# Two cross-attention layers on one core: both Gram products in the middle of a slot, a fixed order for some GpSimd work, and the image values' load and mask at other places

## The chip, the cores and the metric

The kernel runs on one core of one Trainium2 chip. Its time is the device time of one execution in microseconds (us); the time before is the median of three runs. The profile is one further execution, recorded instruction by instruction. The engines are named as the profile names them: PE (TensorE, matmuls; PEld is its weight load), DVE (VectorE), ACT (ScalarE), POOL (GpSimd), SP (SyncE, which issues most DMAs).

## The reference

Two cross-attention layers over a batch of 16 sequences, 256 tokens of 320 channels, 20 heads of 16. The second layer's input is the first layer's output; both attend to the same context (256 tokens of 512 channels per sequence), whose last tokens are "image" tokens with keys and values of their own. Layer 2, which the change is about, cut to what matters:

```python
q = heads(x @ W_q)                       # x: layer 1's output
k_t, v_t = heads(text @ W_k), heads(text @ W_v)     # text: 252 context tokens
probs_t = softmax(q @ k_t.T * 0.25)
text_out = probs_t @ v_t
k_ip, v_ip = heads(ip @ W_k_ip), heads(ip @ W_v_ip) # ip: the last 4 context tokens
qsem = l2norm(probs_t @ text)            # a 512-vector per head and query
sem = qsem @ l2norm(ip).T
probs_ip = softmax(q @ k_ip.T * 0.25 + 0.5 * sem) * spatial_mask
out = (text_out + probs_ip @ v_ip) @ W_out + b_out + x
```

The kernel doesn't form `qsem`. It needs only its norm and its products with the image tokens, and gets both from Gram products of the context: the norm is `p G p`, with `G` the 256 x 256 product of the context with itself and `p` the unnormalized probabilities, and the products with the image tokens are columns of the same `G`.

## The kernel before, in words

Layer 2 goes over 80 slots, `k = NS .. 2*NS - 1` with `NS = 80`: five slots (groups of four heads) for each of the 16 sequences, here called batches. In what follows `n` is the first slot of a batch. Layer 1 fills the 80 slots before in a like manner.

One slot of layer 2 (`slot1`) issues, in this order:

- `both1(k, 0)`: the transposed scores of slot k for the first half of the keys (L788), the plain scores of slot k+2 (L793), whose maximum DVE takes (L794) and whose image columns it copies (L810), and the exponentials on ACT (L800).
- `attend1(k - 2)`: probabilities times values (L861), then the norm's row through a matrix of zeros and ones, the "zone" matmuls (L863), which read the finished norm sum; then `settle1` (L906 to L914).
- `both1(k, 1)`: the same for the second half.
- `norm1(last, 0, 0)`, with `last = k - 1`: four matmuls of the Gram matrix with rounded probabilities (L848) and their product with the low part on DVE (L851).
- side work due by a third of the slot.
- `norm1(last, 0, 1)`, `rounded1(k, 0)`, the loads of a later slot's score operands, `norm1(last, 1, 0)`, `norm1(last, 1, 1)`, `rounded1(k, 1)`: together ten more norm matmuls. Each pair's two products are summed (L853) by POOL for the first pair (`u = 0`) and by DVE for the second. `rounded1` rounds the exponentials of one pair on ACT (L838) and subtracts on POOL (L839) what was rounded off: the "low halves", two of them for each pair. The rounded copies lie in a ring of two buffers, so the copy of slot k takes the place of that of slot k - 1, which the norm matmuls read.
- side work due by two thirds, the maxima's way into the score operands (L826, L828, L830), and side work due by the slot's end.

The side work lies in generators (`task(key, times, ...)`): each has a list of times in slots, and `fill(now)` runs all steps that are due, earliest time first. Those that matter here, with their times against the batch's first slot n:

- `t1`, `tokens1`: two steps for the values (L212), and then one for each of two Gram products of twelve matmuls (also L212, 128x256), with copies by ACT (L487, L488; L493, L494, L498) and DVE (L486, L489; L492, L495, L499). Times -3.67, -3, -2.67, -2.33; a step beyond the list takes the last time.
- `o1`, `open1`: a batch's queries. It loads layer 1's output and splits it into rounded and low parts (`split`: ACT L509, POOL L510, DVE L511) at -7, and projects it (L520 on `hq`) from -6.67 on. L510 is queued. In slots that is the same place at which the batch ahead has just done its Gram products.
- `k1`, `keys1`: a batch's keys, with low parts of the context on POOL (L148 on `cta`), also queued.
- `i1`, `image_softmax`: the image tokens' softmax over all groups of a batch at once, in ten steps from 6.67 to 8.33. Its last lines load the image values of the batch (`vb`, 4 rows of 384, sent to 32 partitions at once; shown as `rs<-vipd`), transpose the probabilities (L960) and multiply `vb` with a mask (L961). `vb` is one tile for all batches.
- `c1`, `close1`: image probabilities times `vb` (L968), the sum with the text part (L969), the output projection (L520 on `ho`) and the store.

Two things set the order of instructions on an engine. PE's order is the program's, as written. For DVE, ACT, POOL and SP a planner in the compiler plays the program through with its own durations and picks, whenever an engine is free, the earliest written instruction that is ready by its reckoning; what waits on a load or on PE can so be overtaken by later work, or later work be put into a gap. Two helpers bind that order: `anchor(inst)` makes `inst` its engine's anchor, replacing the one before, and `queued(inst)` orders `inst` behind its engine's present anchor, without a wait for its result. On the engine itself the order is then fixed, and an instruction that waits holds those behind it.

Of the kernel before, what the change touches and what calls it, by code (L numbers as in the profile page):

```python
# [21 lines left out]
CP = 384  # L22
E = 512
T0 = 77
NIP = 4
# [5 lines left out]
NG = H // 4  # L31
# [10 lines left out]
def RAMP(t):  # L42
    return t if t < -5 or t > 3 else (t + 5) * 0.375
# [5 lines left out]
def xattn2(  # L49
# [27 lines left out]
    nc = tc.nc  # L77
    f = lambda ap: ap.bitcast(F32)
    mm = nc.tensor.matmul

    def dma(out, in_):
        nc.sync.dma_start(*(f(ap) if ap.dtype == FR else ap for ap in (out, in_)))
# [16 lines left out]
    def buf(tag, shape, dtype=F32, bufs=1, name=None):  # L99
        if tag in ("wB", "wD", "vr", "raw"):  # L100
            return sb.tile(shape, dtype, tag=tag, name=name or tag, bufs=bufs)
        size = 1
        for d in shape[1:]:
            size *= d
        if tag not in slots:
            slots[tag] = [0, dtype] + [const_tile([128, max(size, words.get(tag, 0))], f"{tag}_{i}", dtype) for i in range(bufs)]
        n, kind, *ring = slots[tag]
        assert kind == dtype and len(ring) == bufs, tag
        slots[tag][0] += 1
        t = ring[n % bufs][: shape[0], :size]  # L110
        names = "abcd"[: len(shape) - 1]
        if len(names) > 1:
            t = t.rearrange(f"p ({' '.join(names)}) -> p {' '.join(names)}", **dict(zip(names, shape[1:])))
        return t
# [5 lines left out]
    vipd = dram.tile([BI, CP], F32, name="vipd")  # L120
# [11 lines left out]
    def queued(inst, *behind):  # L132

        for other in behind or [anchors.get(inst.ins.engine)]:
            if other is not None:
                tc.add_manual_dep(
                    inst.ins, other.ins.name, mybir.DependencyInfo(mybir.DependencyClass.NoSync, mybir.DependencyReason.DATA), reason="order"
                )
        return inst

    def anchor(inst):
        anchors[inst.ins.engine] = inst
        return inst
# [228 lines left out]
    w1, v1t, gmt = {}, [], []  # L372
# [98 lines left out]
    def tokens1(b):  # L471
        ct = ct1[b]
        V, G = v1t[b % 2], gmt[b % 2]
        vc = vcols(V, V1W)
        for t, lo, sc in ((0, 0, 1.0), (1, DUP, tmask[:, 2:3])):
            vp = bank()[:, :320]
            prod(vp, lambda s, k: ct(s, k)[:, lo : lo + 128], w1["v"], 4)
            nc.scalar.activation(vc[:, t, :, 0:16], vp.rearrange("p (h d) -> p h d", d=D), AF.Copy, scale=sc)
            yield
        rnb = rn[:, 4 * b : 4 * b + 4].unsqueeze(1).to_broadcast([128, H, NIP])  # L480
        for t, lo in ((0, 0), (1, DUP)):
            g = bank()[:, :S]
            prod(g, lambda s, k: ct(s, k)[:, lo : lo + 128], ct, 4)
            ip = g[:, T1:S].unsqueeze(1).to_broadcast([128, H, NIP])
            if t == 0:
                nc.vector.tensor_mul(vc[:, 0, :, 17:21], ip, rnb)  # L486
                nc.scalar.copy(G[:, 0, :], g[:, 0:128])  # L487
                nc.scalar.copy(G[:, 1, 4:], g[:, 128:T1])  # L488
                nc.vector.tensor_sub(G[:, 4, :], g[:, 0:128], f(G[:, 0, :]))  # L489
            else:  # L490
                tm = tmask[:, 2:3]
                nc.vector.scalar_tensor_tensor(vc[:, 1, :, 17:21], ip, tm, rnb, op0=ALU.mult, op1=ALU.mult)  # L492
                nc.scalar.activation(G[:, 2, :], g[:, 0:128], AF.Copy, scale=tm)  # L493
                nc.scalar.activation(G[:, 3, 4:], g[:, 128:T1], AF.Copy, scale=tm)  # L494
                nc.vector.scalar_tensor_tensor(  # L495
                    G[:, 5, :], g[:, 0:128], tm, f(G[:, 2, :]), op0=ALU.mult, op1=ALU.subtract
                )
                nc.scalar.activation(G[:, 5, :], f(G[:, 5, :]), AF.Copy, scale=2.0)  # L498
                nc.vector.scalar_tensor_tensor(  # L499
                    G[:, 6, 4:], g[:, 128:T1], tm, f(G[:, 3, 4:]), op0=ALU.mult, op1=ALU.subtract  # L500
                )
            yield
        return V, G
# [100 lines left out]
    QK, P, W, R = {}, {}, {}, {}  # L604
# [229 lines left out]
    def rounded1(k, u):  # L834
        R[k, u] = buf("ctb", [128, 2, 2, S], FR, bufs=SIZES["CTB"], name="ph")
        W[k, u] = buf("wB", [128, 2, 2, S], bufs=SIZES["WB"], name="wt")
        for t in range(2):
            nc.scalar.activation(R[k, u][:, t], P[k, u][:, t], AF.Copy, scale=0.5)  # L838
            anchor(nc.gpsimd.tensor_sub(W[k, u][:, t], P[k, u][:, t], f(R[k, u][:, t])))  # L839

    blocks = (((0, 0), (2, 1), (4, 0), (5, 1)), ((1, 0), (3, 1), (6, 1)))

    def norm1(k, u, n):

        gm = get("t1", k // NG - B)[1]
        yp = bank().rearrange("p (h t) -> p h t", h=2)
        for i, (gb, kt) in enumerate(blocks[n]):
            mm(yp, gm[:, gb], R[k, u][:, kt], start=i == 0, stop=i == len(blocks[n]) - 1)  # L848
        w = W[k, u]
        product = yp if n and u else w[:, n]  # L850
        nc.vector.tensor_mul(product, yp, w[:, n])  # L851
        if n:
            (nc.vector if u else nc.gpsimd).tensor_add(w[:, 0], w[:, 0], product)  # L853

    def attend1(k):
        b, g = divmod(k - NS, NG)
# [60 lines left out]
    def image_softmax(b, lo=0, hi=NG):  # L917

        gs, n = slice(lo, hi), hi - lo
        nt, si = norms[b][:, gs], results["si", b]  # L920
        pool = nc.gpsimd
        small = lambda n, t: buf(t, [128, NG, 8] + ([n] if n > 1 else []))[:, gs]

        u = small(1, "u")
        pool.tensor_mul(u, nt[:, :, :, 0], nt[:, :, :, 0])
        yield
        nc.vector.scalar_tensor_tensor(u, u, EPS2 / 4, nt[:, :, :, 5], op0=ALU.mult, op1=ALU.max)
        yield
        r = small(1, "r")

        nc.scalar.activation(r, u, AF.Ln, scale=2.0**20)
        nc.scalar.activation(r, r, AF.Exp, bias=w1["shift"], scale=-0.5)
        yield
        b4 = lambda t: t.unsqueeze(3).to_broadcast([128, n, 8, NIP])
        a = small(NIP, "a")
        pool.tensor_mul(a, nt[:, :, :, 1:5], b4(r))
        by_group = lambda t: t[:, :, : NG * NIP].rearrange("p f (g n) -> p g f n", n=NIP)[:, gs]
        pool.tensor_add(a, a, by_group(si))
        yield
        m4 = small(1, "m4")  # L940
        nc.vector.tensor_reduce(m4, a, axis=AX.X, op=ALU.max)
        yield
        pool.tensor_sub(a, a, b4(m4))
        yield
        nc.scalar.activation(a, a, AF.Exp, scale=SCALE)
        yield
        z4 = small(1, "z4")
        nc.vector.tensor_reduce(z4, a, axis=AX.X, op=ALU.add)
        nc.vector.reciprocal(z4, z4)
        yield  # L950
        pool.tensor_mul(z4, z4, mk.unsqueeze(1).to_broadcast([128, n, 8]))
        pi = w1["pip"]
        pool.tensor_mul(by_group(pi), a, b4(z4))
        if hi < NG:
            return
        vb = w1["vb"]
        dma(vb, vipd[NIP * b : NIP * (b + 1)].unsqueeze(0).to_broadcast([32, NIP, CP]))
        yield
        pT = w1["pT"]
        nc.vector.transpose(pT, pi.rearrange("p f c -> p (f c)"))  # L960
        nc.vector.tensor_mul(vb, vb, w1["bmask"])  # L961
        return pT, vb

    def close1(b):
# [28 lines left out]
    def task(key, times, make, *needs):  # L993
        tasks[key] = [times, 0, make, needs, len(tasks)]
# [38 lines left out]
    def shifted(n, *times):  # L1033

        return [RAMP(n + t) for t in times]
# [10 lines left out]
    for c in range(B // 2):  # L1046
        n, k = 10 * c, [("k0", c)] if c else []
# [11 lines left out]
    for b in range(B):  # L1059
        n = NS + 5 * b  # L1060
        task(("k1", b), shifted(n, -7, -6.67, -6.33, -5.67, -5, -4.67), lambda b=b: keys1(b), ("w2",), *([("t1", b - 1)] if b else []), *([("w4", 1)] if b > 2 else []))
        task(("t1", b), shifted(n, -3.67, -3, -2.67, -2.33), lambda b=b: tokens1(b), ("k1", b), ("w3", b % 2))
        task(("o1", b), shifted(n, -7.67, -7, -6.67, -5.33, -4.33, -4), lambda b=b: open1(b), ("w7",), ("c0", b), *([("o1", b - 1)] if b else []))
        task(("i1", b), shifted(n, 6.67, 6.67, 6.67, 6.67, 7.33, 7.33, 7.67, 7.67, 8, 8.33), lambda b=b: image_softmax(b, NG - 1 if b == B - 1 else 0), ("gathered", b), ("taken", B + b - 1), *([("i1a",)] if b == B - 1 else []))
        task(("c1", b), shifted(n + (1.67 if b > B - 3 else 0), 8.67, 9.33, 9.67, 10.33, 11.67, 13.33), lambda b=b: close1(b), ("i1", b), ("w4", 1))
# [160 lines left out]
```

## Time and profile before

| | |
|---|---|
| time, median of 3 runs | 1523.62 us (1520.76 to 1527.41) |
| the profiled execution: time, span | 1525.5 us, 1523.4 us |
| granted TensorE clock, mean | 0.987 |
| PE, PEld busy | 95%, 79% |
| DVE, ACT, POOL busy | 77%, 63%, 75% |
| second half, 760 to 1523 us: PE, POOL, DVE busy | 736.09, 577.18, 635.40 us |
| the longest waits by line | POOL L839 for ACT L838 167.5 us, POOL L679 for ACT L676 161.1 us |

The span is cut into what each engine was busy with; idle time of an engine is put down to what ended it. Rows of the instruction view give the start, the duration, the engine, the line, the operation, the tile written and the tiles read, then in brackets the idle time before and what released it. Rows of the chain give start, duration, engine, tile and line. A row of the waits gives the total, the times it happened and the longest. Matmul ends are modelled. Layer 2's batches repeat with a period of 51.8 us.

### The profile page before, as it was taken

Reading aid. Unit: us, or ns where it says so; the run is one execution under the profiler, and the core shown is the slowest. Engines: PE = TensorE matmul, PEld = TensorE weight load, DVE = VectorE, ACT = ScalarE, POOL = GpSimd, SP = SyncE. Lnnn points to the kernel's source line nnn. Section 1 sums busy time; section 2 is a strip of 40 time slices with the busy share of each in tenths; the row PEclk is TensorE's granted clock in tenths of the full one; section 3 lists DMA queues with packets and bytes.
Section 4 is the critical chain, followed back from the end, with each engine's and each line's share of the span. In section 5 each row is a group of like instructions: output and inputs, shape, how many; then the busy total and the mean of one; then the engine's idle time right before and its main releaser. Section 6 shows DMA issues by size and latency. Waiting matters only on the chain.

```text
span 1523.4 us, 35306 instructions
## 1 busy us (share of the span) xinstructions
PE 1452.4 (95%) x12522; PEld 1196.4 (79%) x12522; DVE 1180.6 (77%) x2584; ACT 956.0 (63%) x2073; POOL 1142.2 (75%) x1161
## 2 busy tenths in 40 slices
PE   7799999999999999799999999999999999999997
PEld 6788888888888878577777877777777777777765
DVE  5467676767676777777888888888888888788896
ACT  5557676767676866656656556656665665556563
POOL 3259797979797967787778678767877787778785
PEclk9899999999999999899999999999999999999999
DMA  6666565656565665465424443443444343434311
GB/s 217 165 176 175 163 175 163 175 162 175 163 175 163 168 182 136 104 188 171 156 86 138 121 139 115 127 130 109 136 117 138 108 144 110 150 98 120 115 42 59
DMA packets 226971, 215.38 MB, mean 141 GB/s; under 512 B 49714, under 2 KB 210708, under 8 KB 226796
## 3 DMA queue, kind: packets, MB, share of 16 engines
q1 hardware_dynamic: 225056, 211.83, 48.4%
q8 instruction: 100, 1.64, 0.5%
q10 hardware_dynamic: 1740, 1.30, 0.3%
q14 instruction: 75, 0.61, 0.2%
HBM read 122.17 MB, written 89.49 MB: 139 GB/s over the span
## 4 chain that ended last, share of the span: by engine, by line
PE 72%; POOL 10%; DVE 6%; DMA 5%; issue 3%; ACT 3%; SPq 0%; ACTq 0%; POOLq 0%; DVEq 0%
PE X L212 21%; PE X L848 14%; PE X L520 10%; PE P L711 7%; POOL wt L839 6%; PE S L650 5%; PE T L673 4%; PE T L788 3%; DMA rs<-vipd 3%; PE P L861 2%; DVE mn L794 2%; PE S L793 2%; POOL wt L853 2%; PE P L863 1%; PE X L569 1%
## 5 line engine op out<-in xcount | busy, mean ns | idle before, releaser
L679 POOL TENSOR_TENSOR P<-P,rs 128x512 f32<-128x512 f32 x320 | 411.4, 1307 | 161.3 <-ACT P L676 161.1
L839 POOL TENSOR_TENSOR wt<-P,ctb 128x512 f32<-128x512 f32 x212 | 271.0, 1292 | 117.7 <-ACT ctb L838 117.7
L848 PE MATMUL X<-ctb,gm 128*128 128x512 f32 x1120 | 293.7, 402 | 0.0
L676 ACT ACTIVATE P<-T 128x512 f32<-128x512 f32 x320 | 174.8, 593 | 106.2 <-PE T L673 99.1
L848 PEld LDWEIGHTS X<-ctb,gm 128*128 128x128 f32 x1120 | 199.5, 188 | 46.4 <-issue 0.4
L794 DVE TENSOR_REDUCE mn<-S 128x4 fp32r<-128x1008 f32 x160 | 191.6, 1197 | 31.3 <-PE S L793 31.3
L851 DVE TENSOR_TENSOR wt<-X,wt 128x512 f32<-128x512 f32 x240 | 164.2, 685 | 31.1 <-PE X L848 30.1
L800 ACT ACTIVATE P<-T 128x512 f32<-128x512 f32 x212 | 114.8, 593 | 47.7 <-PE T L788 47.2
L838 ACT ACTIVATE ctb<-P 128x512 fp32r<-128x512 f32 x212 | 124.2, 625 | 32.0 <-PE X L848 30.5
L652 DVE TENSOR_REDUCE mn<-S 128x4 fp32r<-128x716 f32 x160 | 142.5, 891 | 0.0
L711 PE MATMUL P<-P,vr 128*32 128x256 f32 x1920 | 126.9, 395 | 5.3 <-DVE mx L575 2.8
L520 PE MATMUL X<-hq,wE 128*128 128x256 f32 x768 | 114.4, 292 | 4.7 <-ACT hq L509 3.5
L520 PE MATMUL X<-ho,wF 128*128 128x256 f32 x768 | 108.6, 284 | 4.8 <-DVE ho L752 4.0
L212 PE MATMUL X<-cta,wA 128*128 128x252 f32 (+1 forms) x720 | 105.4, 290 | 7.3 <-ACT wA L147 5.8
L520 PEld LDWEIGHTS X<-hq,wE 128*128 128x128 f32 x768 | 103.6, 194 | 9.1 <-ACT hq L509 4.0
L520 PEld LDWEIGHTS X<-ho,wF 128*128 128x128 f32 x768 | 102.0, 190 | 9.9 <-DVE ho L752 4.4
L839 POOL TENSOR_TENSOR wt<-qsl,ctb 128x512 f32<-128x512 f32 x54 | 69.2, 1293 | 51.9 <-ACT ctb L838 49.8
L853 POOL TENSOR_TENSOR wt<-wt 128x512 f32<-128x512 f32 x80 | 103.3, 1292 | 0.0
L212 PEld LDWEIGHTS X<-cta,wA 128*128 128x128 f32 x720 | 93.8, 194 | 11.9 <-ACT wA L147 6.1
L722 DVE STREAM_TRANSPOSE nt<-P 128x512 f32<-128x512 f32 x80 | 57.1, 713 | 51.9 <-PE P L711 51.9
L147 ACT CAST kst<-X 128x252 fp32r<-128x252 f32 (+3 forms) x94 | 35.1, 373 | 95.3 <-PE X L212 75.5
L711 PEld LDWEIGHTS P<-P,vr 128*32 128x32 f32 x1920 | 56.5, 112 | 46.6 <-issue 9.6
(217 smaller groups left out, 3383.2 us busy)
## 6 DMA issues: line engine op xcount, KB each, us to landing
qd<-q SPq DMA_DIRECT2D x96, 384.0 KB
kd<-kst SPq DMA_DIRECT2D x73, 256.0 KB
rawc<-in_cT_dram SPq DMA_DIRECT2D x60, 256.0 KB
ks<-kd SPq DMA_DIRECT2D x160, 96.0 KB
qs<-qd SPq DMA_DIRECT2D x160, 96.0 KB
qs<-qd SPq DMA_DIRECT2D x60, 192.0 KB
ks<-kd SPq DMA_DIRECT2D x60, 192.0 KB
kd<-kst SPq DMA_DIRECT2D x21, 512.0 KB
```

Source lines behind the costliest of these rows:

```text
L212: last = mm(out, lhs(a, k), rhs(b, k), start=i == 0, stop=i == len(terms) - 1)
L520: mm(pp, w(s, k, slice(m * 128, (m + 1) * 128)), a[:, t], start=i == 0, stop=i == len(terms) - 1)
L652: anchor(nc.vector.tensor_reduce(mn[:, t, 1], sp[:, :, T0:], axis=AX.X, op=ALU.max))
L676: exp = anchor(nc.scalar.activation(pt, st[p], AF.Exp, scale=SCALE))
L679: anchor(nc.gpsimd.tensor_mul(pt, pt, rs[:, t : t + 1].to_broadcast([128, 2, S])))
L711: mm(pv[32 * s : 32 * s + 32, o : o + S], v[:, vt, h : h + 32], P[k, s // 2][:, t, s % 2], start=vt < 2, stop=vt != 1,)
L794: anchor(nc.vector.tensor_reduce(maxes[k + 2][:, t], sp[:, :, :T1], axis=AX.X, op=ALU.max))
L838: nc.scalar.activation(R[k, u][:, t], P[k, u][:, t], AF.Copy, scale=0.5)
L839: anchor(nc.gpsimd.tensor_sub(W[k, u][:, t], P[k, u][:, t], f(R[k, u][:, t])))
L848: mm(yp, gm[:, gb], R[k, u][:, kt], start=i == 0, stop=i == len(blocks[n]) - 1)
L851: nc.vector.tensor_mul(product, yp, w[:, n])
L853: (nc.vector if u else nc.gpsimd).tensor_add(w[:, 0], w[:, 0], product)
```

## The change

The second Gram product of a batch is issued directly after the first, in the middle of slot n-3 (time -2.67 instead of -2.33), so that both stand ahead of the ten norm matmuls of that slot instead of one on each side. The low halves of the second pair (`u = 1`) are queued on POOL, and POOL's norm sum becomes an anchor. The load of the image values is written into the first step of `image_softmax` instead of ahead of its last, and their mask multiplication is queued on DVE.

```diff
@@ rounded1 @@
-            anchor(nc.gpsimd.tensor_sub(W[k, u][:, t], P[k, u][:, t], f(R[k, u][:, t])))
+            low = nc.gpsimd.tensor_sub(W[k, u][:, t], P[k, u][:, t], f(R[k, u][:, t]))
+            anchor(queued(low) if u else low)
@@ norm1 @@
         if n:
-            (nc.vector if u else nc.gpsimd).tensor_add(w[:, 0], w[:, 0], product)
+            total = (nc.vector if u else nc.gpsimd).tensor_add(w[:, 0], w[:, 0], product)
+            if not u:
+                anchor(total)
@@ image_softmax, ahead of its first step @@
+        vb = w1["vb"]
+        if hi == NG:
+            dma(vb, vipd[NIP * b : NIP * (b + 1)].unsqueeze(0).to_broadcast([32, NIP, CP]))
@@ image_softmax, its end @@
         if hi < NG:
             return
-        vb = w1["vb"]
-        dma(vb, vipd[NIP * b : NIP * (b + 1)].unsqueeze(0).to_broadcast([32, NIP, CP]))
         yield
         pT = w1["pT"]
         nc.vector.transpose(pT, pi.rearrange("p f c -> p (f c)"))
-        nc.vector.tensor_mul(vb, vb, w1["bmask"])
+        queued(nc.vector.tensor_mul(vb, vb, w1["bmask"]))
         return pT, vb
@@ the tasks @@
-        task(("t1", b), shifted(n, -3.67, -3, -2.67, -2.33), lambda b=b: tokens1(b), ...
+        task(("t1", b), shifted(n, -3.67, -3, -2.67, -2.67), lambda b=b: tokens1(b), ...
```

More of the change, by code (lines that the diff above doesn't have):

```diff
@@ L1061, in xattn2 @@
         task(("k1", b), shifted(n, -7, -6.67, -6.33, -5.67, -5, -4.67), lambda b=b: keys1(b), ("w2",), *([("t1", b - 1)] if b else []), *([("w4", 1)] if b > 2 else []))
-        task(("t1", b), shifted(n, -3.67, -3, -2.67, -2.33), lambda b=b: tokens1(b), ("k1", b), ("w3", b % 2))
+        task(("t1", b), shifted(n, -3.67, -3, -2.67, -2.67), lambda b=b: tokens1(b), ("k1", b), ("w3", b % 2))
         task(("o1", b), shifted(n, -7.67, -7, -6.67, -5.33, -4.33, -4), lambda b=b: open1(b), ("w7",), ("c0", b), *([("o1", b - 1)] if b else []))
```

## The prediction

> **What bounds the kernel now.** I read the page first (busy shares, then the chain), then a window of one steady batch of layer 2, the chain of waits inside it, the waits by line, and last the instructions in order of time.
>
> ```profile
> PE 1452.4 (95%) x12522; PEld 1196.4 (79%) x12522; DVE 1180.6 (77%) x2584; ACT 956.0 (63%) x2073; POOL 1142.2 (75%) x1161
> PE 72%; POOL 10%; DVE 6%; DMA 5%; issue 3%; ACT 3%; SPq 0%; ACTq 0%; POOLq 0%; DVEq 0%
> ```
> ```profile
> 969.86:1021.67 51.81, 50.65 (x421) 40.24 (x420) 43.45 (x90) 30.87 (x67) 39.19 (x44) 1.00 0.42 125
> ```
>
> The first two lines are the page: TensorE is busy 95% of the span and carries 72% of the chain that ends last. The third is the window of one batch (five slots): the columns after its length are PE, PEld, DVE, ACT and POOL, then the granted clock (1.00). A batch takes 51.81 us and PE is idle for 1.16 us of it, so nothing in this change, which removes no matmul, can win much more than 1.16 us a batch. It can lose more: the chain inside the same batch leaves PE at three places.
>
> ```profile
> 972.71 1.12 PE X L848 x4
> 973.83 1.43 PE X L212 x12
> 975.26 2.32 PE X L848 x10
> 977.59 1.43 PE X L212 x12
> ...
> 979.84 1.21 DVE mn L794
> ...
> 986.75 2.54 POOL wt L839 x2
> ...
> 997.94 2.61 DMA rs<-vipd
> ```
>
> The two L212 x12 are the Gram products of one batch, with the ten norm matmuls L848 between them. Behind them stand a DVE step (979.84), a GpSimd run (986.75) and the load of the image values (997.94). The change touches all three.
>
> **The Gram products.** The second one moves from 977.59 to before the ten norm matmuls. Those then begin 1.43 us later (its piece of the chain). PE's total work is the same, so the next slot's first score matmuls stay where they are, unless an engine is late. The engine that is late is GpSimd. In order of time:
>
> ```profile
> 975.10 2.49 PE L848 MATMUL X<-ctb,gm 128*128 128x512 f32 x10
> 975.59 0.63 ACT L838 ACTIVATE ctb<-qsl 128x512 fp32r<-128x512 f32 x1 [1.04 <-PE X L848]
> 975.60 0.40 DVE L949 RECIPROCAL z<-z 128x40 f32<-128x40 f32 x1
> 976.30 1.29 POOL L839 TENSOR_TENSOR wt<-qsl,ctb 128x512 f32<-128x512 f32 x1 [2.70 <-ACT ctb L838]
> 977.55 0.27 POOL L951 TENSOR_TENSOR z<-z,mk 128x40 f32<-128x40 f32 x1
> 977.78 1.29 POOL L853 TENSOR_TENSOR wt<-wt 128x512 f32<-128x512 f32 x1
> 978.43 0.69 DVE L853 TENSOR_TENSOR wt<-wt,X 128x512 f32<-128x512 f32 x1
> 979.03 1.28 POOL L839 TENSOR_TENSOR wt<-qsl,ctb 128x512 f32<-128x512 f32 x1
> 979.44 0.35 ACT L493 ACTIVATE gm<-X,tmask 128x128 fp32r<-128x128 f32 x1
> 980.27 0.47 POOL L953 TENSOR_TENSOR rs<-a,z 128x160 f32<-128x160 f32 x1
> 980.62 0.61 PE L863 MATMUL P<-wt,zone 128*32 128x256 f32 x8
> 980.70 2.51 POOL L839 TENSOR_TENSOR wt<-ksl,ctb 128x512 f32<-128x512 f32 x2
> 981.79 0.47 PE L788 MATMUL T<-qs,ks 50*128 50x256 f32 x3 [0.24 <-DVE gm L499]
> 983.17 1.31 POOL L510 TENSOR_TENSOR hq<-xq,hq 128x512 fp32r<-128x512 f32 x1
> 984.40 1.23 PE L520 MATMUL X<-hq,wE 128*128 128x256 f32 x8
> ```
>
> The rounding L838 writes a buffer that the norm matmuls still read, so ACT waits (1.04 us) and starts 0.49 us after the ten matmuls start. From there GpSimd runs without a gap from 976.30 to 984.48: low half, L951, norm sum, low half, L953, two low halves, and the low half L510 of the next batch's tokens, which is queued behind them. The query projection L520 starts at 984.40, and its second matmul reads what L510 writes at 984.48: there is no slack at all. So what delays the first low half by 1.43 us delays the projection, less what leaves the run. L951 needs L949, done at 976.00; it then fits into the idle time (2.70 us now) ahead of the first low half and takes 0.25 us (977.55 to 977.78) out of the run. L953 follows L951 and may leave too (0.43 us, 980.27 to 980.70). Bounds for a batch: 1.43 - 0.25 - 0.43 = 0.75 us if both leave; 1.43 + 0.70 = 2.13 us if neither does and the second product's two copies (L493, 0.35 us, and its twin) get ahead of the rounding on ACT. I take 1.18, since L951 was already placed directly behind the first low half and a gate 1.43 us later lets it past, while L953 needs L951's result first.
>
> How often: of the 16 batches, the first has its Gram products in layer 1's last slots, where no such run exists, and the last has no successor whose tokens could wait. **14 x 1.18 = +16.5 us** (10.5 to 29.8).
>
> What else the move does lies under that wait. DVE's norm sum L853 ends 1.43 us later, at 980.55, just as the zone matmuls L863 want it (980.62), and pushes the next maximum by about 0.7 us, up to 0.5 us on PE. In return the second Gram product's copies no longer stand behind the next maximum, where three score matmuls now start at 981.79. Both happen ahead of 984.40, where PE waits for L510 anyway: nothing either way, and 14 x 0.5 = 7 us of loss or gain if that cover were gone. Only the last batch keeps the gain: **-0.5 us**.
>
> **The low halves of the second pair.** As the code stands, the norm sum becomes GpSimd's anchor, but the first pair's low halves, recorded next and not queued themselves, replace it. The second pair is thus queued behind the first pair's last low half, and that order is there already (976.30, 979.03, then x2 at 980.70, the sum at 977.78 ahead). **0 us.** No wait is added for anyone.
>
> **The image values.** The load's tile is single, so its issue on the SP queue, wherever it is written, waits for the last matmuls that read the batch before:
>
> ```profile
> 986.07 0.42 DVE L529 TENSOR_TENSOR q<-X,q 128x256 fp32r<-128x256 f32 x1 [0.98 <-ACT q L528]
> 997.31 0.59 PE L968 MATMUL X<-rs,rs 128*128 128x256 f32 x2
> 997.94 0.53 SPq L82 DMA_DIRECT2D rs<-vipd  x1
> 1000.04 1.28 POOL L839 TENSOR_TENSOR wt<-P,ctb 128x512 f32<-128x512 f32 x1
> 1000.57 1.16 DVE L961 TENSOR_TENSOR rs<-rs,nt 128x384 f32<-128x384 f32 x1 [0.66 <-DMA rs<-vipd]
> 1001.26 0.52 POOL L467 CAST kst<-kip 128x8 fp32r<-128x8 f32 x1
> 1001.66 0.41 DVE L148 TENSOR_TENSOR kst<-X,kst 128x252 fp32r<-128x252 f32 x1
> 1001.99 1.19 DVE L794 TENSOR_REDUCE mn<-S 128x4 fp32r<-128x1008 f32 x1
> 1003.40 0.50 PE L793 MATMUL S<-ks,qs 48*128 48x256 f32 x4 [0.46 <-DVE sr L810]
> 1013.49 0.18 POOL L467 CAST kst<-kip 128x8 fp32r<-128x8 f32 x1
> ```
> ```profile
> DVE rs L961 <- DMA rs<-vipd: 11.8, 15, 1.1
> PE S L793 <- DVE sr L810: 7.4, 15, 0.9
> ```
>
> Issued 0.04 us after PE is done, the load cannot start sooner: the move is worth nothing by itself, and it passes no SP issue that could be held. The mask L961 is what matters. The planner runs it as soon as the load lands, so DVE sits 0.66 us, then multiplies, and the maximum L794 and the copy behind it come late; PE waits for that copy 15 times, 7.4 us in all. Queued behind the score copy three slots further on, L961 meets a load long landed, and DVE is idle there (0.98 us before the query copies, 986.07). If that cover were missing, nothing would ask for it before the image matmuls. What is late next at the old place is L148, 0.41 us: if it still goes ahead of L794, that begins at 1001.65 instead of 1001.99, 0.34 x 15 = 5.1 us won. At most DVE's whole wait for the load comes back, 11.8 us. I take the wait row: **-7.4 us**.
>
> At its new place L961 runs beside GpSimd's L510 or L148. At the old one L839 beside it took 1.28 us, its usual time, and only the tiny L467 grew, 0.52 instead of 0.18. I charge nothing. The Trainium skill (GPSIMD Engine Reference, Key points) says GpSimd shares its SBUF interfaces with VectorE and contends with its instructions that have two SBUF inputs, as L961 has; by it, with the 0.34 us of L467 put on L510, the sum would be 14 x 0.34 = 4.8 us more.
>
> **Sum:** +16.5 - 0.5 + 0 - 7.4 = **+8.6 us**. The profiled execution took 1525.5 us (span 1523.4 and 2.1 around it) and would take 1534.1; it lies 1.9 us above the median of the three runs, so on the median 1523.6 + 8.6 = **1532.2 us**.
>
> **The rivals.** What a measurement of this kernel can tell from no change is about 0.5%, 7.6 us; with the other terms as taken, the delay of L510 decides at 1.11 us a batch.
>
> *Both image steps leave the GpSimd run, and the mask gives its most:* 14 x 0.75 - 0.5 - 11.8 = -1.8, with the taken mask value +2.6: 1521.8 to 1526.2. For it: the idle 2.70 us ahead of the run becomes about 4 us. Against it: the planner now puts L951 behind the first low half although its input was ready 0.3 us before. Same: 0.33 (with the neighbouring values up to +7.6).
>
> *The Gram copies go ahead of the rounding on ACT:* they come earlier in the program. 14 x 2.13 - 0.5 - 5.1 = +24.2: 1547.8. Against it: L493 waits for a matmul group that ends only just ahead of the rounding's gate. 0.13.
>
> *Faster: the rounding is not held by the ten matmuls.* If ACT's 1.04 us in front of L838 is owed to the four norm matmuls before (972.71), which do not move, the first low half stays at 976.30, L510 ends at 984.48, PE waits for it as now, and the mask is won whole: -7.4 - 0.5 = -7.9, 1515.7; with the upper value for the mask -12.3, 1511.3. It decides at a first low half within 0.1 us of today's place in the slot. Against it: L838 follows the start of the ten, long after the four have ended. 0.20, for surprises in the planned order too.
>
> *The change doesn't do what it says* holds for the low halves, and is in the sum.
>
> **How the numbers follow.** The forecast has 0.34, the rival above it 0.13: slower 0.47, same 0.33, faster 0.20. The range runs from 1513, between the faster rival's two values, to 1546, just under the worst case, leaving some 0.08 out at each end.
>
> **What would show it.** Right: the first low half some 1.4 us later after the slot's start, L510 ending about a microsecond later, and a new wait of PE on L510 in the L520 rows, 14 times; L961 without a DMA wait, the 7.4 us of L793 on L810 mostly gone. Wrong: L520 starting where it does now, or the three late score matmuls still waiting on L499.

## The result, and the profile after

The changed kernel took **1536.08 us** (median of four runs, 1533.4 to 1539.41) against 1524.18 us (1520.76 to 1527.41) for the kernel before: ratio **1.0079, 95% interval 1.005 to 1.0109**, slower, as forecast, by 11.9 us where 8.6 were worked out. The profiled execution took 1536.06 us, span 1534.3. Its page, the two lines that answer to those of before:

```profile
PE 1458.9 (95%) x12522; PEld 1198.9 (78%) x12522; DVE 1191.9 (78%) x2584; ACT 952.2 (62%) x2073; POOL 1143.0 (74%) x1161
PE 72%; POOL 16%; DVE 3%; ACT 3%; DMA 3%; issue 2%; SPq 0%; ACTq 0%; POOLq 0%; DVEq 0%
```

On the chain, GpSimd went from 10% to 16%, and DMA (the load ahead of the mask) from 5% to 3%. The window of one batch, columns as before, and then the Gram slot in order of time (it starts at 973.7 here, at 969.86 before, so 3.8 is to be taken off for comparing):

```profile
988.31:1040.55 52.24, 50.88 (x421) 40.19 (x419) 44.25 (x91) 30.68 (x67) 39.28 (x44) 1.00 0.43 125
```
```profile
979.90 0.27 POOL L957 TENSOR_TENSOR z<-z,mk 128x40 f32<-128x40 f32 x1 [2.45 <-DVE z L955]
980.25 0.47 POOL L959 TENSOR_TENSOR rs<-a,z 128x160 f32<-128x160 f32 x1
980.36 2.48 PE L849 MATMUL X<-ctb,gm 128*128 128x512 f32 x10
980.84 0.63 ACT L838 ACTIVATE ctb<-qsl 128x512 fp32r<-128x512 f32 x1 [0.86 <-PE X L849]
981.55 1.30 POOL L839 TENSOR_TENSOR wt<-qsl,ctb 128x512 f32<-128x512 f32 x1 [0.83 <-ACT ctb L838]
...
987.78 1.30 POOL L510 TENSOR_TENSOR hq<-xq,hq 128x512 fp32r<-128x512 f32 x1
987.79 1.88 DVE L965 TENSOR_TENSOR rs<-rs,nt 128x384 f32<-128x384 f32 x1
988.31 0.28 PE L520 MATMUL X<-hq,wE 128*128 128x256 f32 x1
989.14 1.09 PE L520 MATMUL X<-hq,wE 128*128 128x256 f32 x7 [0.55 <-POOL hq L510]
989.18 1.64 POOL L148 TENSOR_TENSOR cta<-rawc,cta 128x512 fp32r<-128x512 f32 x1
```

The first low half L839 comes 1.4 us later in the slot (981.55 against 976.30), since ACT's rounding L838 still waits for the ten norm matmuls. Both image steps (L957 and L959, the former L951 and L953) now stand ahead of the run. The run ends with L510 at 989.08, 0.8 us later in the slot; one matmul of the projection L520 starts and the other seven wait 0.55 us for it. The waits by line say how often:

```profile
PE X L520 <- POOL hq L510: 7.9, 13, 1.4
PE S L793 <- DVE sr L810: 3.9, 15, 0.7
```

PE waits for L510 13 times: twelve times 0.53 to 0.55 us, and once, at 780.42, 1.4 us, where the kernel before waited 0.7. The sum of its waits for the maxima's copy L810 fell from 7.4 us to 3.9, but these are not the same waits. The one behind the mask's old place (0.46 us at 1003.40 before) is gone. The ones that are left in the steady batches, 0.22 us each, stand in the Gram slot (985.89), where the kernel before has none; run 1 below, with the Gram time alone, has them too. The mask no longer waits for its load.

To sum this up over the layer I took the starts of L509, the cast of a batch's tokens. Their last twelve distances are 51.76 us before and 52.19 us after in the mean, 5.2 us in all. The batch ahead of these took 54.47 us instead of 50.27: 4.2 us in one place. The start of the layer came out 2.1 us earlier, and the end, from the last L509 on, 3.5 us longer. That makes the 10.9 us between the spans, but for rounding. The prediction has only the first of these items.

The one place, in the changed kernel and then in the kernel before:

```profile
739.89 0.28 PE L826 MATMUL X<-ident_r,mn 128*4 128x128 f32 x2
740.51 1.03 ACT L147 CAST wF<-rawc 128x384 fp32r<-128x384 f32 x2 [2.23 <-DMA rawc<-in_wo_dram]
742.75 0.36 ACT L828 CAST mt<-X 4x256 fp32r<-4x256 f32 x1
743.16 1.65 PE L212 MATMUL X<-cta,wA 128*128 128x252 f32 x12 [2.99 <-ACT mt L828]
```
```profile
741.42 0.28 PE L826 MATMUL X<-ident_r,mn 128*4 128x128 f32 x2
741.54 1.59 PE L212 MATMUL X<-cta,wA 128*128 128x252 f32 x12
742.68 0.36 ACT L828 CAST mt<-X 4x256 fp32r<-4x256 f32 x1
```

The keys' matmuls L212 read `cta` and `wA`, not `mt`; nothing they compute needs L828. Before, they start ahead of it. After, they wait 2.99 us for it, behind a cast that waits for a load of weights. What they share with L828 is a PSUM bank (the X tiles, which the matmuls write, are given places in banks of PSUM): in the compiled program of the changed kernel this keys' tile has the bank of the L826 tile directly before it, which L828 reads; in the kernel before it has not. In the compiled program the first of these matmuls waits for the signal that L828 sets; in the kernel before it waits for a norm product instead (L851). The planner that orders the instructions also hands out the banks, and in the programs compared here a change in the order changed which earlier tile's bank a tile got.

### The profile page after: what moved, and what is told of

Read it like the earlier page. It is cut to its first block, busy times and chain, and to the rows that moved or that the text cites. A ratio compares the mean times of both kernels' runs of the same rounds, so it can differ in the third digit from the quotient of the medians.

```text
span 1534.3 us, 35366 instructions
## 1 busy us (share of the span) xinstructions
PE 1458.9 (95%) x12522; PEld 1198.9 (78%) x12522; DVE 1191.9 (78%) x2584; ACT 952.2 (62%) x2073; POOL 1143.0 (74%) x1161
## 4 chain that ended last, share of the span: by engine, by line
PE 72%; POOL 16%; DVE 3%; ACT 3%; DMA 3%; issue 2%; SPq 0%; ACTq 0%; POOLq 0%; DVEq 0%
PE X L212 22%; PE X L849 11%; PE X L520 10%; POOL wt L839 9%; PE P L711 7%; PE S L650 5%; PE T L673 4%; PE P L864 3%; PE T L788 3%; POOL wt L854 3%; PE S L793 2%; PE P L866 2%; ACT ctb L838 1%; PE X L569 1%; POOL hq L510 1%
## 5 line engine op out<-in xcount | busy, mean ns | idle before, releaser
L839 POOL TENSOR_TENSOR wt<-P,ctb 128x512 f32<-128x512 f32 x212 | 270.7, 1293 | 97.4 <-ACT ctb L838 97.4
L794 DVE TENSOR_REDUCE mn<-S 128x4 fp32r<-128x1008 f32 x160 | 191.7, 1198 | 25.0 <-PE S L793 25.0
L838 ACT ACTIVATE ctb<-P 128x512 fp32r<-128x512 f32 x212 | 124.0, 624 | 29.9 <-PE X L849 29.1
L520 PE MATMUL X<-hq,wE 128*128 128x256 f32 x768 | 116.0, 293 | 11.7 <-POOL hq L510 7.9
L520 PEld LDWEIGHTS X<-hq,wE 128*128 128x128 f32 x768 | 103.7, 194 | 17.6 <-POOL hq L510 10.6
L520 PE MATMUL X<-ho,wF 128*128 128x256 f32 x768 | 110.8, 288 | 4.0 <-DVE ho L752 2.5
L212 PE MATMUL X<-cta,wA 128*128 128x252 f32 (+1 forms) x720 | 104.7, 289 | 9.5 <-ACT wA L147 5.1
L520 PEld LDWEIGHTS X<-ho,wF 128*128 128x128 f32 x768 | 104.0, 194 | 9.6 <-DVE ho L752 3.0
L212 PEld LDWEIGHTS X<-cta,wA 128*128 128x128 f32 x720 | 93.1, 193 | 14.1 <-ACT wA L147 5.4
L854 POOL TENSOR_TENSOR wt<-wt 128x512 f32<-128x512 f32 x80 | 103.0, 1288 | 0.0
L839 POOL TENSOR_TENSOR wt<-qsl,ctb 128x512 f32<-128x512 f32 x54 | 69.2, 1294 | 43.1 <-ACT ctb L838 41.0
L651 DVE TENSOR_REDUCE mn<-S 128x4 fp32r<-128x308 f32 x160 | 74.7, 467 | 23.7 <-PE S L650 23.4
```

Source lines behind the costliest of these rows:

```text
L212: last = mm(out, lhs(a, k), rhs(b, k), start=i == 0, stop=i == len(terms) - 1)
L520: mm(pp, w(s, k, slice(m * 128, (m + 1) * 128)), a[:, t], start=i == 0, stop=i == len(terms) - 1)
L794: anchor(nc.vector.tensor_reduce(maxes[k + 2][:, t], sp[:, :, :T1], axis=AX.X, op=ALU.max))
L839: low = nc.gpsimd.tensor_sub(W[k, u][:, t], P[k, u][:, t], f(R[k, u][:, t]))
L854: total = (nc.vector if u else nc.gpsimd).tensor_add(w[:, 0], w[:, 0], product)
```

## The experiments

Each ratio is against the kernel before, timed on the same chip. Below, a "period" is the median of the last twelve distances of L509. The waits of PE are those of the window from 930 to 1340 us, about eight batches: total, times, longest.

**1. The Gram time alone.** In the kernel before, only

```
-task(("t1", b), shifted(n, -3.67, -3, -2.67, -2.33), ...
+task(("t1", b), shifted(n, -3.67, -3, -2.67, -2.67), ...
```

> Only the Gram products side by side. Theory (the GpSimd run that ends in L510 is held by the ten norm matmuls, and the query projection waits for L510): about +10 us against the kernel before (14 batches by some 0.7 us), with a wait of PE on L510 of about 0.5 us a batch. Rival (the loss comes from the mask multiplication, which at its new place runs beside GpSimd and takes longer): +3 us or less, and little waiting for L510.

Measured: 1545.34 us, ratio 1.0119 (1.0096 to 1.0142), 17.9 us; period 52.56 against 51.76 before, and 53.91 in the one batch. PE's waits, before and then here (a wait of 0.4 us a batch of L863 for L853 stands in both):

```profile
PE S L793 <- DVE sr L810: 3.7, 8, 0.5
PE T L788 <- DVE gm L499: 2.0, 8, 0.2
```
```profile
PE S L793 <- DVE sr L810: 5.7, 16, 0.8
PE X L520 <- POOL hq L510: 4.3, 8, 0.6
```

The wait for L510 is there as foretold (0.54 us a batch); the wait for L499 went, and a second wait for the maxima's copy came in its place. L510 ends 15.41 us after the slot's start here and 14.62 before, so 0.79 us later, and the batch is 0.79 us longer. The profiled spans differ by 19.4 us: the last twelve distances take 13.4 us more (12 x 0.79 = 9.5, 2.8 more in one batch of 55.38 us at a granted clock of 0.97, 1.2 more in the first), the one batch 3.6 more, with a stall of 2.6 as in the changed kernel, the end 3.5 more, and the start 1.1 less.

**2. The queued mask alone.**

```
-        nc.vector.tensor_mul(vb, vb, w1["bmask"])
+        queued(nc.vector.tensor_mul(vb, vb, w1["bmask"]))
```

> Only the mask multiplication queued on DVE. Theory: DVE no longer waits for the image values, the scores of the first slot of each batch follow 0.35 us sooner: about -5 us against the kernel before. Rival (the mask is the cost): +3 us or more, with the mask at over 1.5 us each and L510 or L148 beside it longer.

Measured: 1527.84 us, ratio 1.0001 (0.9985 to 1.0017); period 51.93. No gain, although the mask's wait for its load is gone, and PE's wait for L810 behind the old place with it. The waits for L810 in the first of these views are others: 0.31 us in the slot after the mask's new place (989.65).

```profile
PE X L212 <- DVE ho L752: 5.3, 8, 0.7
PE S L793 <- DVE sr L810: 2.7, 8, 0.6
PE T L788 <- DVE gm L499: 1.7, 7, 0.2
```
```profile
995.62 0.59 PE L968 MATMUL X<-rs,rs 128*128 128x256 f32 x2
997.41 0.47 DVE L752 SCALAR_TENSOR_TENSOR ho<-ho,tmask,X 128x256 fp32r<-128x256 f32 x1
997.93 1.64 PE L212 MATMUL X<-cta,wA 128*128 128x252 f32 x12 [0.66 <-DVE ho L752]
```

Again the keys' matmuls wait for a reader of a tile that they don't use: L752 splits the image tile of L968, and in this program the keys' tile gets that tile's bank, three tiles on. In the kernel before it has the bank of a norm tile (L848) five tiles back, long read. The first matmul's wait in the compiled programs says the same: for L752's signal here, for the norm product L851's before.

**3. Low halves and load alone.** The first three hunks of the change's diff and the removal of the old load.

> The GpSimd queue of the second pair's low halves and the place of the load, without the Gram products' place and without the mask's queue. Theory: nothing, within 3 us of the kernel before. Rival (the new order on GpSimd holds a low half or L510 back): +5 us or more, with longer waits of the zone matmuls on GpSimd.

Measured: 1526.0 us, ratio 1.0 (0.998 to 1.002). These two parts are worth nothing, as costed.

**4. The changed kernel with the projection a third of a slot later.**

```
-task(("o1", b), shifted(n, -7.67, -7, -6.67, -5.33, -4.33, -4), ...
+task(("o1", b), shifted(n, -7.67, -7, -6.33, -5.33, -4.33, -4), ...
```

> The changed kernel with the first part of the query projection a third of a slot later (time -6.33 instead of -6.67), behind the ten norm matmuls, about 2.3 us more for GpSimd. Theory: PE's wait for L510 goes, 8 to 10 us below the changed kernel, about the kernel before or a little under it (1520 to 1528). Rival (the loss lies elsewhere): within 3 us of the changed kernel.

Measured: 1540.81 us, ratio 1.0098 (1.0063 to 1.0134). The wait for L510 is gone and the time is not. Its keys' tile has the image tile's bank (13 waits for L752, 8.6 us), and in four batches PE waits for the mask, 10.9 us in all. In those four the mask takes 5.6 us instead of 1.7:

```profile
882.70 5.59 DVE L965 TENSOR_TENSOR rs<-rs,nt 128x384 f32<-128x384 f32 x1
882.71 1.30 POOL L510 TENSOR_TENSOR hq<-xq,hq 128x512 fp32r<-128x512 f32 x1
883.96 0.21 POOL L910 COPY tmp<-nt 128x48 f32<-128x48 f32 x1
884.14 1.29 POOL L148 TENSOR_TENSOR cta<-rawc,cta 128x512 fp32r<-128x512 f32 x1
885.39 2.48 POOL L839 TENSOR_TENSOR wt<-qsl,ctb 128x512 f32<-128x512 f32 x2
888.43 0.81 PE L972 MATMUL X<-rs,rs 128*128 128x256 f32 x2 [2.71 <-DVE rs L965]
```

The mask ends 0.4 us behind the fifth of five GpSimd instructions in a row. The seven executions of this kernel spread from 1533 to 1551 us; whether the number of such batches makes that spread is not shown. As a test of the L510 wait the run decides nothing. The runs that follow have the norm tile's bank for the steady keys' tile.

**5. The queued mask with the bank free.** The mask as in 2, and the last time of `i1` 8 instead of 8.33, which moves the mask into the Gram slot and leaves the keys' tile the norm tile's bank.

> The kernel before with the mask multiplication queued, as in the run with the queued mask alone, but with the last time of the image softmax 8 instead of 8.33, so that its last step (the transposition and the mask) comes a third of a slot earlier. What this is for: in the run with the mask alone, the keys' tile of L212 had been given the PSUM bank of the image tile hp three tiles after it, and PE waited for its reader L752 (18 us by the waits); with this edit the tile gets the bank of a norm tile five tiles back, as in the kernel before. Theory (the queued mask is worth 0.35 to 0.5 us a batch, and the bank took it back): no PE wait on L752, no wait of the mask on its load, 5 to 7 us faster than before (ratio 0.995 to 0.997). Rival (the queued mask wins nothing in this order of work): within 2 us of before.

Measured: **1514.06 us, ratio 0.9914 (0.9889 to 0.994)**; period 51.06, 0.7 less than before. The longest wait left in the window, and the mask:

```profile
PE P L863 <- POOL wt L853: 2.8, 8, 0.4
```
```profile
972.03 0.55 DVE L961 TENSOR_TENSOR rs<-rs,nt 128x384 f32<-128x384 f32 x1
```

The waits for L810 (0.46 us a batch) and for L499 (0.25) are both gone: 0.71, which is the period. More than expected, because the L499 wait went too; DVE's L499 now stands ahead of L810 in the planned order. Against run 2 three things differ at once, the bank, the mask's slot (where it takes its 0.55 us beside no GpSimd work) and that order, so the 0.7 us are not the bank's alone. (The expectation's 18 us add the waits of PE, 7.9, and of its weight load, 10.2, which overlap.)

**6. The time of 5 without the queue.** The kernel before with the last time of `i1` at 8.

> The kernel before with the last time of the image softmax 8 instead of 8.33 and nothing queued: the first half of the edit of the run that gave 0.9914. Theory (the gain comes from the queued mask, which now runs three slots later in DVE's idle time, beside no GpSimd work and with the keys' tile in a bank of its own): the time alone leaves the order of every engine as in before, so within 2 us of before, with PE's wait of L793 on L810 still there 15 times. Rival (the earlier step is itself the gain): 1512 to 1518.

Measured: 1525.21 us, ratio 0.9997 (0.9977 to 1.0017). The time alone leaves the compiled order of every engine as it was, and does nothing; the gain of 5 needs the queued mask.

**7. The Gram time alone, L510 on VectorE.** As 1, and `nc.vector` for `nc.gpsimd` in the split of the queries.

> The kernel before with the Gram time alone (the second product directly behind the first) and the low half L510 on VectorE. The Gram time alone gave a ratio of 1.0119. Theory (the wait for L510): no wait of PE on L510, 7 to 10 us of the 18 come back (ratio 1.005 to 1.008); the rest is what the image load's maximum costs (S tiles of L793 on L810), which this edit leaves. Rival (all of the 18 us hang on L510's lateness): ratio 0.998 to 1.003. Rival (none does): 1.010 to 1.014.

Measured: 1533.31 us, ratio 1.0044 (1.0026 to 1.0063), 12 us below run 1; period 51.92, and 50.27 in the one batch.

```profile
PE S L793 <- DVE sr L810: 5.4, 16, 0.5
```

No wait for L510 is left in the window, and the batch is 0.64 us shorter than in run 1 (52.56 - 51.92). The keys' tile of the one place has another bank here, and its stall is gone with it. What is left of the Gram time is 0.16 us a batch.

**8. The changed kernel with the last time of `i1` at 8**, the control for the next run.

> Control for the two runs beside it: the changed kernel with the last time of the image softmax 8 instead of 8.33 and nothing else. Both theories: this edit by itself changes neither the Gram slot nor a bank, so ratio 1.005 to 1.011 as for the changed kernel. Rival (an earlier transposition and mask help or hurt by themselves): a ratio outside of that, which would then have to be taken off the other two.

Measured: 1535.66 us, ratio 1.0048 (1.0029 to 1.0067); period 52.20, as the changed kernel's, and 55.54 in the one batch, whose bank is the changed kernel's. But by another wait:

```profile
PE P L866 <- DVE wt L854: 5.6, 8, 0.7
PE P L866 <- POOL wt L854: 3.1, 8, 0.4
```

The zone matmuls L866 read DVE's norm sum L854, which is late. With the mask in the Gram slot the planned order on DVE has the maximum L794 ahead of that sum; in the changed kernel the sum is first (983.86, then L794 at 984.46). Here:

```profile
984.18 1.20 DVE L794 TENSOR_REDUCE mn<-S 128x4 fp32r<-128x1008 f32 x1
985.29 0.67 DVE L854 TENSOR_TENSOR wt<-wt,X 128x512 f32<-128x512 f32 x1
```

PE is late before it reaches L520, and finds L510 done.

**9. Run 8 with L510 on VectorE.**

> The changed kernel with the low half of the queries (L510) on VectorE instead of GpSimd, so that it no longer stands behind the run of low halves, and with the last time of the image softmax 8 instead of 8.33, which keeps the bank of the keys' tile away from hp's. Theory (PE's wait for L510 is what the Gram order costs, 0.5 to 0.7 us in 13 batches): that wait is gone and the time is 6 to 10 us below the changed kernel's, at the time before or a little under it (ratio 0.995 to 1.002), unless VectorE, with 0.7 us more in that slot, delays the next maximum. Rival (the cost is elsewhere, in the late norm sum and the zone matmuls): ratio as the changed kernel's, 1.006 to 1.011.

Measured: 1537.28 us, ratio 1.006 (1.0038 to 1.0083), no gain; period 52.56, though the one-place stall is gone (50.32).

```profile
PE P L866 <- DVE wt L854: 8.3, 8, 1.0
```

With the norm sum late already, removing L510 from GpSimd frees nothing, and DVE is later still. The expectation took L510 for the only wait of that slot; run 8 shows another in its place.

**10. All of the change but the Gram time**, with the last time of `i1` at 8.

> The changed kernel with the Gram time put back to -2.33 and the last time of the image softmax at 8: low halves, load and mask of the change, without its Gram part. Theory (the Gram order costs 0.8 us a batch and low halves and load are worth nothing): as the queued mask with the bank free, 1512 to 1518 (ratio 0.989 to 0.994), that is 18 to 23 us below the changed kernel with the same last time (ratio 1.0048), without a PE wait on L510 or on the DVE norm sum L854. Rival (low halves or load carry part of the loss once the mask is in place): 1519 to 1528.

Measured: 1514.99 us, ratio 0.9919 (0.9891 to 0.9948); period 51.06. Against run 8 only the Gram time differs: ratios of 1.0048 and 0.9919, some 20 us. Low halves and load add nothing to run 5. Runs 5 and 10 are faster than both kernels; 5 is the smaller edit.

The banks in the compiled programs, and what PE's keys' matmuls L212 wait for in the whole span (total, times):

| kernel | bank of the keys' tile, steady batch | in the one place | waits for L752, us | for L828, us | the one batch, us |
|---|---|---|---|---|---|
| before, 3, 6, 10 | norm tile's, five back | another | none | none | 49.65 to 50.27 |
| after | norm tile's | L826 tile's, one back | none | 3.0, 1 | 54.47 |
| 1 Gram alone | norm tile's | L826 tile's | none | 2.6, 1 | 53.91 |
| 8 control | norm tile's | L826 tile's | none | 2.9, 1 | 55.54 |
| 2 mask alone | image tile's, three back | another | 7.9, 12 | none | 49.76 |
| 4 late projection | image tile's | another | 8.6, 13 | none | 50.29 |
| 5 mask, bank free | norm tile's | another | none | none | 49.75 |
| 7 Gram, L510 on DVE | norm tile's | another | none | none | 50.27 |
| 9 run 8, L510 on DVE | norm tile's, but one image tile's | another | 0.7, 1 | none | 50.32 |

The waits stand where the keys' tile has the bank of the image tile that L752 reads or, in the one place, of the L826 tile directly before it, and nowhere else. The counts agree too: of the thirteen such tiles of the steady batches twelve have the image tile's bank in run 2, thirteen in run 4 and one, the one that waits, in run 9. No run changed a bank and left every order as it was: the same order got the same banks. That the bank is the cause rests on this table, on the waits written into the compiled programs, and on the waiting instruction having no other tie to the releaser. What the stall in the one place is worth by itself is known only as the wait, 2.6 to 3.0 us; the batch there is 3.6 to 5.3 us longer.

## Why the prediction was right

**The mechanism of the Gram term held.** Rounding held by the ten matmuls, the GpSimd run later, L510 late, PE waiting in L520: each is in the rows above, 13 times where 14 were counted (and one of the 13 was there before, shorter), and run 7 removes it.

**Its size was off, and what else it cost was left out.** The step that failed is "I take 1.18, since ... L953 needs L951's result first": both image steps left the run, so L510 ends 0.78 us later in the slot, about the lower bound of 0.75, and a batch of run 1 is 0.79 us longer. That is 14 x 0.79, some 11 us, and not 16.5. Only 0.54 us of it shows as a wait for L510, since PE comes to L520 late already. Yet the Gram time alone cost 17.9. The batch with the shared bank in one place took 3.6 us more, which no term had; about 3 us are left, and how they divide among slow clock, start and end of the layer the single profile does not show. What the prediction put under the cover of L510's wait was real, but small in sum. The next maximum is late, and PE waits for its copy 0.2 us a batch in runs 1 and 7 (the second wait for L810). With L510 gone, the zone matmuls took 17.3 us in five batches against 15.6 before, 0.34 us a batch, and 1.8 us came back on L788, no longer held by L499; 0.16 us a batch is what remains of it all:

```profile
L788 PE MATMUL T<-qs,ks 50*128 50x256 f32 x200 | 27.0, 332 | 1.2 <-DVE gm L499 1.2
L863 PE MATMUL P<-wt,zone 128*32 128x256 f32 x200 | 15.6, 384 | 2.0 <-POOL wt L853 2.0
```
```profile
L788 PE MATMUL T<-qs,ks 50*128 50x256 f32 x200 | 25.2, 330 | 0.0
L863 PE MATMUL P<-wt,zone 128*32 128x256 f32 x200 | 17.3, 386 | 1.9 <-POOL wt L853 1.9
```

(Groups of PE by line, five batches: busy, mean ns, and idle before them; the kernel before, then run 7.)

**The mask.** -7.4 was taken. Beside the Gram change it gave 0.36 us a batch (period 52.56 in run 1, 52.20 after), 15 x 0.36 = 5.4, just above the lower bound of 5.1: L148 does stay ahead of L794, which begins 0.96 us after the start of the score matmuls that it reads (1005.30 to 1006.26), where it was 1.31 (1000.68 to 1001.99). By itself it gave nothing, and in run 5, with the bank free and the mask in another slot, 0.7 us a batch. The term's size belonged to the kernel that it stood in.

**Low halves and load at 0** held (runs 3 and 10). **The last batch's -0.5** did not show; the end became longer, of which 2.1 us is the clock (below).

**Contention.** The prediction charged nothing for the mask beside L510. It gave 4.8 us as the price if L510 paid what the tiny L467 had paid, which is how it read the contention that the Trainium skill states (GPSIMD Engine Reference, Key points). There is contention, but L510 does not pay it:

```profile
L965 DVE TENSOR_TENSOR rs<-rs,nt x16: 557/1701/1882, 779.2 to 1517.5; 128x384 f32<-128x384 f32 x16
L510 POOL TENSOR_TENSOR hq<-xq,hq x29: 1250/1300/1487, 120.4 to 1405.4; 128x512 fp32r<-128x512 f32 x29
```

(Least, median and most ns.) The mask needs 0.56 us alone and 1.70 in the median, L510 its usual 1.30. The mask starts within 0.02 us of L510's start and ends 0.4 us behind L510's end in ten of twelve batches. In those ten GpSimd's next instruction, the copy L910, takes 0.55 to 0.58 us instead of 0.22. In the slot shown above and in one more, L910 takes 0.24, the mask ends later, and L148 behind it takes 1.6 us instead of 1.29. So the instruction that is second pays, first the mask and then a GpSimd instruction that finds the mask at work. The Trainium skill (SBUF — State Buffer, "SBUF: two separate sides") has it that the pair of ports is locked for the whole instruction by whichever of the two starts first; these rows agree. No wait of PE in the window from 930 to 1340 us names the mask, so the sum without the 4.8 us was the better one here. That it was harmless is luck of this order: in run 4 the same mask took 5.6 us in four batches and PE waited 10.9 us for it.

So the total, 11.9 us against 8.6, came out near partly by luck: a Gram term some 5 us too large and a mask term 2 us too large stood beside 4.2 us in one place and a longer end, which the sum did not contain.

## What to carry to other kernels

When the waiting instruction has no use for what its releaser makes, look for a buffer or a PSUM bank that the two share; where a planner hands out banks, any reordering can create or remove such a wait far from the edit, and an edit that "gives nothing" may have paid for one. Before pricing a run of queued work by who leaves it, see which small steps become ready in the idle time that the delay opens ahead of it. Before you queue work of VectorE beside a run of GpSimd work, look at how long it takes there in every batch, and not only in one. And try the parts of a change apart: here one part was worth 13 us in the right place, and another cost 18.

## What the runs showed of the hardware that was not expected

The last projection is the same 23 matmuls in both kernels, and took 3.13 us before and 5.27 after. The windows around it (length, PE, PEld, DVE, ACT, POOL, granted clock), before and after:

```profile
1516.00:1519.30 3.30, 3.13 (x23) 2.86 (x23) 1.76 (x6) 0.12 (x1) 0.00 (x0) 1.00 0.27 96
```
```profile
1524.80:1530.10 5.30, 5.27 (x23) 4.98 (x23) 1.64 (x4) 0.03 (x1) 0.00 (x0) 0.52 0.09 30
```

The granted clock is 1.00 in the one and 0.52 in the other, though PE had idled about as long ahead of it (3.02 us before, 2.79 after, both for the last transposition of the image probabilities). Run 3, whose time is that of the kernel before, ends like the changed kernel (5.27 us for the 23 at 0.50), and run 5, the fastest, has a slow end too (4.63 us for 24 matmuls at 0.69). So the slow end does not belong to the change, and 1 to 2 us of a single profiled span hang on it. What sets it is not shown.

A VectorE instruction can be held through several GpSimd instructions in a row: the mask of run 4 took 5.6 us instead of 0.56 in four batches, beside five of them.
